# A second level of Strassen's scheme in one projection of a graph attention layer, and a layer norm made in its input's buffer

## The chip, the cores and the metric

The kernel runs on one core of a Trainium2 chip. The metric is device time in microseconds (us), the median over several executions. Engines are named as in the profile: PE is TensorE, PEld its weight load, DVE VectorE, ACT ScalarE, POOL GpSimd, SP SyncE. Where a kernel was timed several times all its runs were in the fast state (a run alone, "one look" below, has no state of its own); the runs of one kernel on one chip agreed within 0.2%.

## The reference, cut to what matters

```python
h = relu(layernorm(x))                       # x: 128 x 64 x 512, fp32
heads = [attend(h, W_heads[i]) for i in 0..3]         # FIRST projection, 4 heads
h1 = elu(concat(heads))                               # 8192 rows x 2048
o  = elu(attend(h1, W_out))                           # SECOND projection, 2048 -> 512
y  = relu(o @ w1 + b1) @ w2 + b2 + o                  # feed forward
out = x + layernorm(y) * gamma + beta
```

`attend` multiplies by the weights, makes a 64x64 softmax from scores and mixes the rows with it. The 8192 rows are worked on as 16 groups (0 to 15) of 512.

## The kernel before

Each group's matrix products use one level of Strassen's scheme (Winograd's form): 7 products of half-size blocks in place of 8. The second projection sums each of the 7 over four heads, with a 256-column moving operand:

```python
def project2(g):
    slot = {1: "11", 2: "12", 3: "12", 4: "22", 5: "S1", 6: "11", 7: "S1"}
    ...
    def post(what, a, b=None, to=None):
        behind = {"s1": ("11", "S1", "11"), "s5": ("S1", "22", "11"), "c11": ("12", "12", "11")}
        if what in behind:                     # the next operands, in place, behind a product
            dst, x0, x1 = (h1[n] for n in behind[what])
            for h in range(H):
                nc.gpsimd.tensor_tensor(dst[:, h], x0[:, h], x1[:, h], ALU.subtract)
        ...
    return unit(f"b{g}", product_n(ms, lambda p, i: h1[slot[p]][:, i]), post, (1, 5, 6, 2, 7, 3, 4))
```

While TensorE does that, the program mixes three other jobs in: the layer norm of group g+2, the z products (softmax weights times rows) of group g+1, and the feed forward of group g-1. Their small steps go through all engines.

```python
rstd = ...; nc.gpsimd.tensor_tensor(rstd, ve, mhalf, ALU.pow)            # A: 1/sqrt of a variance, GpSimd
nc.scalar.activation(HN[t], X.pop(t), AF.Relu, bias=nb, scale=rstd)      # B: layer norm, ScalarE, needs A
nc.scalar.copy(dst, srcv)                                                # C: z out of PSUM, ScalarE
nc.vector.scalar_tensor_tensor(y, y, rstd, xr, ALU.mult, ALU.add)        # D: last norm, VectorE, needs A
eng.tensor_tensor(dst, a, dst, ALU.add)                                  # E: feed forward out of PSUM, VectorE
```

## Time and profile before

| | before |
|---|---|
| median of 3 runs | 2365.08 us |
| TensorE busy | 98% of the span |
| one group in the steady state | 143.0 us |
| waits of TensorE in the steady state | none |

Busy time in one stretch of 600 us (PE, PEld, DVE, ACT, POOL, then the clock, the DMA share and GB/s):

```profile
PEclk7999999999999999999999999999999999999999
```

```profile
L639 DVE SCALAR_TENSOR_TENSOR jf<-wh,ao 128x512 f32<-128x512 f32 x128 | 94.3, 776 | 40.3 <-ACT wh L621 40.1
```

```profile
1000.00:1600.00 600.00, 600.00 (x3078) 503.06 (x3078) 331.60 (x561) 233.62 (x417) 257.56 (x224) 1.00 0.46 151
```

TensorE never pauses in the stretch, and its clock is full after the start. GpSimd works 257.56 of 600 us, 43%. VectorE is 55% busy.

### The profile page before, as it was taken

The numbers are of one execution on the slowest core, as the hardware profiler recorded it, in microseconds if no ns is written. First come the engines' busy times: TensorE is split into PE (matmuls) and PEld (weight loads), VectorE is DVE, ScalarE is ACT, GpSimd is POOL, SyncE is SP. The second block draws the span as 40 slices with busy tenths as digits, with TensorE's granted clock in tenths as the row PEclk, the third lists the DMA queues.
The fourth block names the chain that finished last, engine by engine and source line by source line (L and its number), as shares of the span: only waits on it lengthen the run. The fifth ranks groups of instructions, "written<-read, shape, count | busy, mean of one in ns | idle before, by whom it ended". The sixth has DMA issues, their size and how long they took to land.

```text
span 2360.4 us, 32849 instructions
## 1 busy us (share of the span) xinstructions
PE 2317.9 (98%) x11805; PEld 1934.5 (82%) x11805; DVE 1265.5 (54%) x2210; ACT 911.0 (39%) x1623; POOL 1026.7 (43%) x917
## 2 busy tenths in 40 slices
PE   6989999999999999999999999999999999999997
PEld 4868787888878888787887878888788887878885
DVE  7625474554646556474554745556464563744527
ACT  2524425253352533425244251533525344251513
POOL 5664444416344353443524444253443534533333
PEclk7999999999999999999999999999999999999999
DMA  8545353444535445353444544435354453534443
GB/s 308 184 142 193 125 183 127 164 152 132 182 125 178 134 139 179 126 180 129 154 163 129 182 131 161 153 130 181 127 177 132 138 179 127 182 118 164 157 148 106
DMA packets 257809, 366.89 MB, mean 155 GB/s; under 512 B 22216, under 2 KB 145128, under 8 KB 257648
## 3 DMA queue, kind: packets, MB, share of 16 engines
q1 hardware_dynamic: 251024, 343.82, 43.9%
q0 software_dynamic: 4512, 16.78, 1.9%
q10 hardware_dynamic: 2112, 4.19, 0.5%
q8 instruction: 95, 1.56, 0.3%
q14 instruction: 66, 0.54, 0.1%
HBM read 337.45 MB, written 27.26 MB: 155 GB/s over the span
## 4 chain that ended last, share of the span: by engine, by line
PE 94%; DVE 2%; ACT 1%; POOL 1%; issue 0%; DMA 0%; DVEq 0%
PE g_b L322 33%; PE g_a L307 32%; PE g_c L307 8%; PE g_d L322 8%; PE pz L525 4%; PE pa L673 2%; PE pto L700 1%; PE pzS L525 1%; PE pth L371 1%; PE s1pt L472 1%; PE pf L381 1%; PE s1pe L406 1%; DMA x<-in_x_dram 0%; PE s2pt L667 0%; PE pwa L193 0%
## 5 line engine op out<-in xcount | busy, mean ns | idle before, releaser
L322 PE MATMUL g_b<-w,h 128*128 128x256 f32 x2560 | 598.1, 381 | 0.0
L322 PEld LDWEIGHTS g_b<-w,h 128*128 128x128 f32 x2560 | 480.5, 190 | 72.2 <-issue 10.1
L307 PE MATMUL g_a<-z,w 128*128 128x256 f32 x1520 | 361.0, 380 | 1.2 <-DVE g_a L581 0.7
L307 PE MATMUL g_a<-zs_z,w 128*128 128x256 f32 x1504 | 347.9, 379 | 0.0
L307 PEld LDWEIGHTS g_a<-z,w 128*128 128x128 f32 x1520 | 287.6, 190 | 57.9 <-issue 14.3
L307 PEld LDWEIGHTS g_a<-zs_z,w 128*128 128x128 f32 x1504 | 284.8, 190 | 50.5 <-issue 14.3
L322 PE MATMUL g_b<-w,hS 128*128 128x256 f32 x1024 | 243.5, 382 | 0.0
L585 POOL TENSOR_TENSOR hS<-hS,h 128x512 f32<-128x512 f32 x64 | 83.0, 1297 | 366.8 <-DVE hS L549 366.8
L547 ACT ACTIVATE exc<-g_a 128x512 f32<-128x512 f32 x256 | 152.3, 595 | 199.7 <-DVE g_a L581 119.6
L322 PEld LDWEIGHTS g_b<-w,hS 128*128 128x128 f32 x1024 | 191.4, 191 | 30.9 <-issue 6.7
L549 DVE SCALAR_TENSOR_TENSOR h<-exc,g_a 128x512 f32<-128x512 f32 x192 | 131.6, 686 | 136.3 <-ACT exc L548 136.2
L548 ACT ACTIVATE exc<-exc 128x512 f32<-128x512 f32 x256 | 161.6, 631 | 6.5
L615 POOL TENSOR_TENSOR h<-h,h 128x512 f32<-128x512 f32 x64 | 86.7, 1362 | 138.1 <-PE g_b L322 138.0
L332 POOL TENSOR_TENSOR zs_z<-zS,z 128x512 f32<-128x512 f32 x63 | 89.7, 1424 | 128.3 <-PE g_a L307 123.7
L615 POOL TENSOR_TENSOR h<-hS,h 128x512 f32<-128x512 f32 x64 | 81.1, 1268 | 142.4 <-PE g_b L322 142.4
L474 ACT COPY at<-s1pt 128x512 f32<-128x512 f32 x64 | 34.7, 588 | 279.8 <-PE s1pt L472 279.8
L307 PE MATMUL g_c<-ot,w 128*128 128x256 f32 x512 | 123.9, 385 | 0.8 <-DVE n2ve L347 0.8
L322 PE MATMUL g_d<-w,rt 128*128 128x256 f32 x512 | 121.5, 380 | 1.7 <-DVE o L740 1.0
L307 PE MATMUL g_a<-zS,w 128*128 128x256 f32 x496 | 117.2, 379 | 0.0
L639 DVE SCALAR_TENSOR_TENSOR jf<-wh,ao 128x512 f32<-128x512 f32 x128 | 94.3, 776 | 40.3 <-ACT wh L621 40.1
L333 POOL TENSOR_TENSOR zs_z<-z,zs_z 128x512 f32<-128x512 f32 x63 | 85.4, 1357 | 61.1 <-PE g_a L307 40.7
L307 PEld LDWEIGHTS g_c<-ot,w 128*128 128x128 f32 x512 | 93.9, 190 | 21.8 <-issue 9.3
(159 smaller groups left out, 3535.6 us busy)
## 6 DMA issues: line engine op xcount, KB each, us to landing
w<-tc SPq DMA_DIRECT2D x632, 256.0 KB, 2.6
w<-in_L_gnn_W_heads_dram SPq DMA_DIRECT2D x192, 256.0 KB, 2.7
w<-in_L_gnn_W_out_dram SPq DMA_DIRECT2D x192, 256.0 KB, 2.7
w<-in_L_gnn_w_dram SPq DMA_DIRECT2D x96, 256.0 KB, 2.7
x<-in_x_dram SPq DMA_DIRECT2D x66, 256.0 KB, 3.6
xr<-in_x_dram SPq DMA_DIRECT2D x64, 256.0 KB, 2.8
out_dram<-o SPq DMA_DIRECT2D x64, 256.0 KB, 2.1
tc<-pt POOLq DMA_DIRECT2D x20, 512.0 KB, 5.6
```

The lines of the kernel that those rows point to most:

```text
L307: nc.tensor.matmul(bk[:, o, :], w[:, k, ts(o, P)], a[:, k, :], start=start and o == 0 and k == 0, stop=k == 1, skip_group_check=True,)
L322: nc.tensor.matmul(bk[:, j, :], a[:, k, ts(j, P)], w[:, k, :], start=start and k == 0 and j == 0, stop=i == len(ms) - 1 and k == 1, skip_g ...
L332: eng.tensor_tensor(s2, s1, a11, ALU.subtract)
L333: eng.tensor_tensor(s4, a12, s2, ALU.subtract)
L525: nc.tensor.matmul(banks[b][:, c, :].rearrange("p (h n) -> p h n", h=H), src[rows, off + c * P:off + (c + 1) * P], at[rows, b], start=True ...
L547: nc.scalar.activation(ex, src, AF.Relu, scale=-1.0)
L548: nc.scalar.activation(ex, ex, AF.Exp, scale=-1.0)
L549: nc.vector.scalar_tensor_tensor(dst, ex, -1.0, src, ALU.add, ALU.max)
L585: nc.gpsimd.tensor_tensor(dst, dst, H1["22"][:, h], ALU.add)
L615: nc.gpsimd.tensor_tensor(dst[:, h], x0[:, h], x1[:, h], ALU.subtract)
L639: nc.vector.scalar_tensor_tensor(junk, WH2[g][:, j], 1.0, ao[:, c, :], ALU.mult, ALU.mult, accum_out=f[:, c, j:j + 1],)
L673: nc.tensor.matmul(pa, AT2[g][:, j, :], WH2[g][:, j, :], start=True, stop=True)
```

## The change

The intent: in groups 3 to 15 each of the 7 products of the second projection is itself done by Strassen's scheme, 49 products of 128x128 blocks in place of 56. That saves an eighth of TensorE's streaming there. It costs sums: differences of quarter blocks of h1 in every group, sums of the result, and, once, sums of the blocks of W_out (made on GpSimd in groups 1 to 3, stored to HBM). To make room, the layer norm is written over x in x's own buffer.

```diff
-        HN[t] = big.tile([P, F], FP, tag="hn", name=f"hn{t}", bufs=G)
-        nc.scalar.activation(HN[t], X.pop(t), AF.Relu, bias=nb, scale=rstd)
+        HN[t] = X.pop(t)
+        nc.scalar.activation(HN[t], HN[t], AF.Relu, bias=nb, scale=rstd)
...
+    def block_sums(p, i):                       # once: groups 1 to 3, 14 units
+        ... two loads of y on GpSimd's queue
+        nc.gpsimd.tensor_tensor(t[:, 0], y12, y11, ALU.subtract)
+        ... three more, and a store
...
+            if g >= DEEP and h == H - 1:        # half sums of h1, 4 a group
+                for n in {"c11": ["11"], "c12": ["12"], "c21": ["S1", "22"]}.get(what, []):
+                    q = H1[n][:, :, :, P:]
+                    nc.gpsimd.tensor_tensor(q[:, :, 0], q[:, :, 0], q[:, :, 1], ALU.add)
...
+    def project2_deep(g):
+        outer = (1, 2, 5, 6, 3, 7, 4)
+        halves = ((6, 7, 5), (3, 1, 2, 4))
+        def quarter_sums(p):                    # 21 a group
+            nc.gpsimd.tensor_tensor(q2, x[:, :, 0, P:], x[:, :, 0, :P], ALU.subtract)
+            nc.gpsimd.tensor_tensor(q3, x[:, :, 1, P:], q2, ALU.subtract)
+            nc.gpsimd.tensor_tensor(q4, x[:, :, 1, :P], q2, ALU.subtract)
+        ...
+        def part(p, half, j):                   # one of the 49 products
+            ...
+                    if half == 1:
+                        behind(h1, p)           # the 12 old differences, after outer products 1, 2, 5
+                        if p == 3:
+                            inner(0, nc.gpsimd) # 5 sums of the result's upper half
+                        if p == 4:
+                            inner(1, nc.vector) # and of its lower half
+                if j == 3 and p != outer[-1]:
+                    quarter_sums(outer[outer.index(p) + 1])
...
-                prefetch(2 * p + 2)             # the loads of x move to the last z product that
-                prefetch(2 * p + 3)             # reads the buffer; the norms move later
...
+            if g <= DEEP:
+                ... 14 block_sums spread over the first projections of groups 1 to 3
```

Also, several scratch tiles get one buffer where they had two (`s1`, `s5`, `t`), and the ring of weight pieces has 10 buffers where it had 11.

## The prediction

> **What bounds the kernel now.** I read the page first, then the waits of TensorE, the groups of matmuls with their shapes kept apart, the timeline of two stretches, and busy time by stretch. The page gives the span, the chain and the groups that the change touches:
>
> ```profile
> span 2360.4 us, 32849 instructions
> PE 2317.9 (98%) x11805; PEld 1934.5 (82%) x11805; DVE 1265.5 (54%) x2210; ACT 911.0 (39%) x1623; POOL 1026.7 (43%) x917
> ...
> PE 94%; DVE 2%; ACT 1%; POOL 1%; issue 0%; DMA 0%; DVEq 0%
> ...
> L322 PE MATMUL g_b<-w,h 128*128 128x256 f32 x2560 | 598.1, 381 | 0.0
> ...
> L322 PE MATMUL g_b<-w,hS 128*128 128x256 f32 x1024 | 243.5, 382 | 0.0
> ```
>
> The reader is to see that TensorE is 94% of the chain that ended last, and that the second projection (g_b, 3584 instructions) has no idle time ahead of it. An fp32 product of two 128x128 blocks is two instructions: 16 groups x 7 products x 16 calls = 1792 calls, 3584 records. The waits of TensorE confirm it; the longest are all single ones of the start:
>
> ```profile
> PE pzS L525 <- DVE z L537: 5.5, 1, 5.5
> PE s1pt L472 <- DVE s1A L435: 5.4, 1, 5.4
> PE pab L158 <- DMA ar<-in_L_gnn_a_heads_dram: 5.4, 1, 5.4
> ```
>
> Busy time can't say how fast matmuls stream, since ends are modelled (a mean of 381 ns is longer than their spacing). The timeline can, where chunks of 8 follow each other:
>
> ```profile
> 1201.43 1.70 PEld L307 LDWEIGHTS g_a<-z,w 128*128 128x128 f32 x8
> ...
> 1203.16 1.70 PEld L307 LDWEIGHTS g_a<-zS,w 128*128 128x128 f32 x8
> ...
> 1204.88 1.70 PEld L307 LDWEIGHTS g_a<-z,w 128*128 128x128 f32 x8
> ```
>
> 8 instructions in 1.725 us: 216 ns for 256 columns, with no loss between products. The steady state is therefore pure streaming. The first g_b products of two neighbouring groups start at 956.3 and 1099.25 us: 143.0 us a group.
>
> **What the Trainium skill says.** "TensorE: Matmul & The Clock Gate", Step-by-step, says that the next weights are loaded while this matmul runs, and LDWEIGHTS (loading the stationary operand) that a load costs time by its columns, not by the matmul's width. This decides the case: halving the moving width to 128 columns leaves the weight load as it is, so the load could become the bound. The trace agrees with both, and lets me size it:
>
> ```profile
> 985.41 1.04 PE L371 MATMUL pth<-ident,hn 128*128 128x128 f32 x8
> ...
> 30.31 3.96 PEld L193 LDWEIGHTS pwa<-aT,wT 128*128 128x128 f32 x18
> ```
>
> Transposes of 128 columns: (1.04 - 0.27) / 7 = 109 ns apart, so 128 columns stream in 109 ns. The second line is from the start: full 128-column fp32 weights, but matmuls only 2 wide, so it is the load alone: (3.96 - 0.33) / 17 = 213 ns, at a granted clock of 0.50 in that stretch, 107 ns at full clock. So load and stream are nearly equal at 128 columns; I expect 109 to 111 ns, and the load to stay hidden, just.
>
> "GPSIMD Engine Reference", Specifications, says that GpSimd shares its SBUF interface with VectorE and contends with VectorE's instructions of two SBUF inputs. The trace agrees: the same 128x512 addition takes 1268 ns in one group (L615 h<-hS,h) and 1424 ns in another (L332), the means below.
>
> ```profile
> L615 POOL TENSOR_TENSOR h<-hS,h 128x512 f32<-128x512 f32 x64 | 81.1, 1268 | 142.4 <-PE g_b L322 142.4
> L332 POOL TENSOR_TENSOR zs_z<-zS,z 128x512 f32<-128x512 f32 x63 | 89.7, 1424 | 128.3 <-PE g_a L307 123.7
> ```
>
> "DMA: Bandwidth & Descriptors", Specifications, puts the size from which a descriptor runs at line rate at 512 B. The new pieces of uncombined blocks have runs of exactly 512 B (128 floats); no group of the trace before shows such a load in bulk.
>
> **The change part by part.**
>
> 1. Streaming. Groups 3 to 15 (13 of 16) take the deep form. Before: 112 calls of 256 columns, 224 x 0.216 = 48.4 us a group. After: 49 x 4 = 196 calls of 128 columns, 392 x 0.109 = 42.7 us. Saved: 5.7 us a group, 13 x 5.7 = 74 us. If the load adds 2 ns, 392 x 2 ns x 13 = 10 us of that goes.
>
> 2. GpSimd work in every deep group: 21 sums of quarter blocks (128x512), 4 sums into the H1 quadrants (128x512), 5 inner sums of the results (two of 512, three of 256 elements). At 1.3 us and 0.75 us: 27.3 + 5.2 + 4.8 = 37 us. It is not spread: it falls on the stretch of the second projection. Before, that stretch (first row) has 48.8 us of GpSimd in 91.8 us, the next one only 11.7 in 51.1:
>
> ```profile
> 956.30:1048.10 91.80, 91.80 (x504) 76.14 (x503) 50.76 (x82) 28.38 (x51) 48.80 (x44) 1.00 0.46 153
> 1048.10:1099.20 51.10, 51.10 (x232) 43.54 (x231) 27.36 (x52) 28.31 (x50) 11.69 (x9) 1.00 0.45 149
> ```
>
> So about 86 us of GpSimd in a stretch of about 86 us. Not all of the 48.8 us must end inside it, but GpSimd goes from a helper to nearly the bound there. I followed the order of both engines' instructions through one group with these durations: with 1.3 us a sum GpSimd keeps ahead except at one place, with 1.4 us it also falls behind at the last outer product (1.4 us), with 1.45 us by 2.7 us. I take 0.7 us a group for the late part: 12 x 0.7 = 8 us.
>
> 3. The one place where it is always late: the first inner product of a group needs a difference of quarters of h11, which waits for the last head's ELU and for the sum of h11's quarters. From the trace, the product ends at 1095.96, ELU at 1097.98:
>
> ```profile
> 1094.07 1.89 PE L307 MATMUL g_a<-z,w 128*128 128x256 f32 x8
> 1095.80 3.62 PE L307 MATMUL g_a<-zs_z,w 128*128 128x256 f32 x16
> 1099.25 1.03 PE L322 MATMUL g_b<-w,h 128*128 128x256 f32 x4
> ...
> 1097.29 0.69 DVE L549 SCALAR_TENSOR_TENSOR h<-exc,g_a 128x512 f32<-128x512 f32 x1 [0.70 <-ACT exc L548]
> ```
>
> Two GpSimd sums after it, 2 x 1.3, end at 1100.6, while TensorE wants to start at 1099.25 (third line). 1.4 us, and 0.1 us for the weight load then exposed: 1.5 us x 13 = 20 us.
>
> 4. The last group has no other work for TensorE beside most of its inner products. GpSimd's share there, some 27 (quarters) + 16 (12 old sums of h) + 4 (H1) + 5 (inner) + 5 (bias) = 57 us, meets about 50 us of TensorE: 8 us lost, more than that group saves.
>
> 5. Block sums of the weights, once, in groups 1 to 3: 14 units, each with loads and a store issued on GpSimd, four sums of 256 elements, and a wait for its own load in GpSimd's order: 4 x 0.75 + 4 x 0.7 (an issue cost 0.58 to 0.79 us before) + about 2 us of wait = 8 us, 112 us in all, while the first projection needs its sums z. Its slack is about one head (12 us), so I charge 10 us.
>
> 6. DMA: 49 pieces of 256 KB instead of 28, and 10 buffers instead of 11. Queue 1 moved 343.8 MB at 43.9% of the engines' time: 332 GB/s at full use. A deep group of 86 us takes (49 + 14 + 12) x 0.262 = 19.7 MB, 229 GB/s, or about 70%. The ring still reaches 9 pieces x 0.87 us = 7.8 us ahead, against 2.6 us to landing. No charge.
>
> 7. The first layer norm in x's own buffer removes 2 of 4 small buffers and moves loads; TensorE didn't wait there before, so nothing is gained or lost.
>
> Sum: -74 + 20 + 8 + 8 + 10 = -28 us: 2365 - 28 = **2337 us**.
>
> **The rivals.** (a) The weight load isn't hidden at 128 columns. For it: load and stream are equal, any handover shows. Against: the loads of pwa follow each other without a gap. At 115 ns 31 us go and little gain stays; at 130 ns 107 us go: about 2440 us, slower. (b) GpSimd keeps up everywhere, and the first sum is early enough: then only parts 4 and 5 cost, some 2309 us, 2.4% faster. The slack of GpSimd's idle time before L332 speaks for it, the chain of part 3 against. (c) GpSimd is the bound of the stretch, by contention with VectorE, which gets more additions too: 4 to 6 us a group lost in all, the gain is used up, 2365 us. (d) DMA: runs of 512 B stream at a lower rate and pieces come late; at 1 us a piece the 75 transfers still fit into 86 us, so only the last group would suffer, some 5 us.
>
> **Range and chances.** The gain can't exceed 74 us (2291), and parts 3 and 4 alone take 28 of it, so over 2% (under 2318) needs one of them to fail: 0.20. Rival (c) reaches 2365, a part of (a) also. Eight in ten: 2308 to 2366. Slower by over 2% needs (a) in full: 0.04. Within 2%: 0.76.
>
> **What would show it.** Spacing of the 128-column g matmuls in the timeline: 109 to 111 ns right, 115 or more rival (a). Waits of TensorE: a wait for GpSimd at a difference of quarters, some 13 times 1.5 us at the start of a deep group; none means (b), many over all outer products means (c). GpSimd's busy share in the stretch near 90% or more. A group's period about 143 - 5.7 + 1.5 + 0.7 = 139.5 us. In groups 1 to 3, waits for the sums z on GpSimd, some 10 us. A wait of TensorE for w from DMA would show (d). The prediction is wrong if the period of deep groups stays at 143 us or falls under 138 us.

## The result, and the profile after

| | before | after |
|---|---|---|
| median (4 runs each) | 2364.63 us | 2620.55 us (2619.28 to 2624.04) |
| ratio, 95% interval | | 1.1085 (1.1066 to 1.1105) |
| one deep group, in the steady state | 143.0 us | 160.3 us (157.7 to 162.0) |
| groups 1 and 2 | 143.0, 143.0 us | 165.9, 161.3 us |

A ratio is the mean time of one kernel's runs over that of the other's in the same rounds, so it isn't quite the ratio of the medians in the table. A group's time is measured from the first transpose of o (`pto`) in one group to that in the next, and averaged over nine steady groups.

The change was predicted at 2337 us and made the kernel 10.9% slower. From the page of the kernel after:

```profile
span 2619.1 us, 38669 instructions
PE 2360.9 (90%) x13989; PEld 2037.7 (78%) x13989; DVE 1377.4 (53%) x2314; ACT 928.4 (35%) x1688; POOL 1596.4 (61%) x1405
...
PEclk7999989999999999999999999999999999999999
...
PE 63%; POOL 19%; DVE 9%; issue 6%; ACT 2%; DMA 2%; POOLq 0%; SPq 0%; DVEq 0%; ACTq 0%
...
L743 PE MATMUL g_b<-wq,q 128*128 128x128 f32 x2184 | 307.9, 286 | 41.7 <-POOL q L690 24.6
```

TensorE fell from 94% to 63% of the chain that ended last, and GpSimd holds 19% of it. Yet GpSimd is only 61% busy over all, and the products that read its quarter differences (last line) wait for the difference q only 24.6 us in the whole run, as part 3 of the prediction had it. So where are the other waits? The waits of TensorE (us in total, times, longest):

```profile
PE g_d L380 <- DVE o L901: 81.8, 25, 8.5
PE pz L580 <- ACT z L590: 36.4, 11, 3.4
PE g_b L743 <- POOL q L690: 24.6, 15, 4.0
...
PE s1pe L464 <- POOL R L450: 16.3, 11, 1.5
PE g_b L743 <- POOL n2rs L407: 16.1, 11, 1.6
```

The two largest are not in the projection that was changed, and they don't name GpSimd. They are the second feed-forward product (`g_d`), which waits for VectorE to take a sum out of PSUM (step E), and the z product (`pz`), which waits for ScalarE to do the same (step C). The timeline tells who held these two up. First the z product of one group, all engines (start, length, what; in brackets the idle time before and its releaser):

```profile
1394.77 4.95 POOL L670 TENSOR_TENSOR h<-hS,h 128x512 f32<-128x512 f32 x4 [0.23 <-PE g_b L743]
...
1396.61 1.13 PE L580 MATMUL pz<-at,hn 64*128 64x256 f32 x8
...
1396.84 0.15 DVE L405 TENSOR_SCALAR n1ve<-n1mv 128x1 f32<-128x1 f32 x1
...
1402.12 0.55 POOL L407 TENSOR_TENSOR n1rs<-n1ve,mhalf 128x1 f32<-128x1 f32 x1
...
1403.07 0.81 ACT L417 ACTIVATE hn<-hn,n1nb,n1rs 128x512 f32<-128x512 f32 x1 [5.75 <-POOL n1nb L415]
1403.79 0.56 ACT L590 COPY z<-pz 128x512 f32<-128x512 f32 x1
```

```profile
1404.41 1.13 PE L580 MATMUL pz<-at,hn 64*128 64x256 f32 x8 [3.38 <-ACT z L590]
```

Read it backwards from the last line. TensorE waited 3.38 us for a PSUM bank that ScalarE had to empty. The products to be copied had begun at 1396.61 and lasted 1.13 us, so the copy could have run at 1397.7. It ran at 1403.79, because ScalarE's queue had the layer norm (step B) ahead of it and stood 5.75 us there. Step B needed step A, a half-microsecond instruction whose input was ready at 1396.99 (third line) and which ran at 1402.12. GpSimd was busy all this time: four differences issued in one go (4.95 us), then two further sums. TensorE thus waited for ScalarE, which waited for GpSimd.

The second feed-forward product of the same group, a little later:

```profile
1460.82 1.71 POOL L729 TENSOR_TENSOR wh<-wh 128x512 f32<-128x512 f32 x1 [0.27 <-DVE wh L719]
...
1461.33 0.14 DVE L405 TENSOR_SCALAR n2ve<-n2mv 128x1 f32<-128x1 f32 x1
...
1462.48 1.71 POOL L690 TENSOR_TENSOR q<-h 128x512 f32<-128x512 f32 x1
1464.16 0.72 POOL L730 TENSOR_TENSOR wh<-wh 128x256 f32<-128x256 f32 x1
1464.84 0.55 POOL L407 TENSOR_TENSOR n2rs<-n2ve,mhalf 128x1 f32<-128x1 f32 x1
...
1465.42 1.20 DVE L910 SCALAR_TENSOR_TENSOR o<-o,n2rs,xr 128x512 f32<-128x512 f32 x1 [2.34 <-POOL n2rs L407]
...
1466.55 0.68 DVE L901 TENSOR_TENSOR o<-g_d,o 128x512 f32<-128x512 f32 x1
...
1467.28 3.68 PE L380 MATMUL g_d<-w,rt 128*128 128x256 f32 x8 [5.14 <-DVE o L901]
...
1470.79 2.40 PE L743 MATMUL g_b<-wq,hS 128*128 128x128 f32 x20
```

It is the same pattern through another queue. The variance is ready at 1461.47, step A runs at 1464.84, behind two inner sums of the result and one quarter difference. VectorE stands 2.34 us at step D, and the evacuation E (L901), for which TensorE waits 5.14 us, is queued behind D. Two more things are to be seen here. The first two sums on GpSimd took 1.71 us in place of 1.27, and both overlap work of VectorE. (From 650 to 2300 us none of the 142 sums of this size that ran with VectorE idle took over 1.29 us, and all 116 of 1.65 us or more overlap VectorE. Not every overlap slows a sum.) And the 8 instructions of `g_d` (256 columns each) took 3.68 us after the wait, where 8 of that size took 1.89 us in the timeline before (the prediction's part 3): the clock had been halved. The stretches show both (columns as above; the first is the 600 us that were shown of the kernel before):

```profile
1000.00:1600.00 600.00, 549.26 (x3382) 478.47 (x3383) 309.43 (x518) 226.59 (x415) 368.25 (x308) 0.96 0.58 168
```

```profile
1460.00:1475.00 15.00, 9.86 (x66) 9.01 (x65) 11.41 (x15) 0.00 (x0) 14.65 (x13) 0.89 0.65 183
```

In the 15 us of the second, GpSimd works 14.65 us: it is the bound of that place, though its mean over the 600 us is 61%. ScalarE did nothing at all in them.

The last two lines of the list of waits are 1.5 us a group each. Before `s1pe`, TensorE waits for R, an operand of a later group's scores, which GpSimd makes behind other sums, as it does step A (in this group its input is ready at 1431.74, and R runs at 1434.89, behind a block of four differences and a quarter difference). The other wait is put down to step A (`n2rs`), and wrongly:

```profile
1478.01 0.68 DVE L721 TENSOR_TENSOR wh<-g_b,wh 128x512 f32<-128x512 f32 x1
...
1478.79 1.13 PE L743 MATMUL g_b<-wq,q 128*128 128x128 f32 x8 [1.60 <-POOL n2rs L407]
```

In all 11 of these waits the product of the last outer product starts 0.10 us after the end of VectorE's evacuation L721, and 0.28 us after the end of the step A that the list names. By these times TensorE waits for VectorE, which has score products (`jf`) ahead of L721.

Two passages of the Trainium skill bear on this. "TensorE: Matmul & The Clock Gate", Architectural detail, says that ScalarE and VectorE take their instructions strictly in order, and that only TensorE can draw something ahead (its weight loads). The timelines agree: a copy that was ready at 1397.7 stood 6.1 us behind a layer norm that wasn't. The same page, Part 1, says that the clock is either full or half, and changes in windows of about 3.4 us. The trace agrees with that: all 23 half-clock stretches from 650 to 1940 us lasted 3.4 or 6.8 us.

Where the 258.7 us between the two spans (2360.4 and 2619.1) come from, by the first transposes of o:

| part | us |
|---|---|
| start, up to the first transpose of o (246.3 to 257.9) | +11.6 |
| groups 1 and 2 (143.0 to 165.9 and 161.3) | +41.2 |
| groups 3 to 13, eleven of them, 17.1 each | +188.5 |
| group 14 (135.9 to 140.6) | +4.7 |
| group 15 (77.8 to 88.5) | +10.7 |
| tail (41.9 to 43.5) | +1.6 |

### The profile page after: what moved, and what is told of

Same layout as the page of the kernel before. It is cut to its first block, busy times and chain, and to the rows that moved or that the text cites. A ratio compares the mean times of both kernels' runs of the same rounds, so it can differ in the third digit from the quotient of the medians.

```text
span 2619.1 us, 38669 instructions
## 1 busy us (share of the span) xinstructions
PE 2360.9 (90%) x13989; PEld 2037.7 (78%) x13989; DVE 1377.4 (53%) x2314; ACT 928.4 (35%) x1688; POOL 1596.4 (61%) x1405
## 4 chain that ended last, share of the span: by engine, by line
PE 63%; POOL 19%; DVE 9%; issue 6%; ACT 2%; DMA 2%; POOLq 0%; SPq 0%; DVEq 0%; ACTq 0%
PE g_a L365 27%; PE g_b L743 13%; PE g_c L365 7%; PE g_b L380 4%; PE pz L580 4%; DVE jf L797 3%; POOL q L690 3%; POOL h L670 3%; PE g_d L380 3%; POOL hS L670 2%; PE pa L832 2%; POOL n2rs L407 1%; DVE o L910 1%; PE pth L429 1%; PE s1pt L530 1%
## 5 line engine op out<-in xcount | busy, mean ns | idle before, releaser
L743 PE MATMUL g_b<-wq,q 128*128 128x128 f32 x2184 | 307.9, 286 | 41.7 <-POOL q L690 24.6
L743 PEld LDWEIGHTS g_b<-wq,q 128*128 128x128 f32 x2184 | 278.3, 198 | 73.8 <-POOL q L690 30.5
L743 PE MATMUL g_b<-wq,h 128*128 128x128 f32 x2080 | 277.6, 285 | 0.0
L743 PEld LDWEIGHTS g_b<-wq,h 128*128 128x128 f32 x2080 | 265.3, 200 | 15.6 <-issue 6.3
L380 PEld LDWEIGHTS g_d<-w,rt 128*128 128x128 f32 x512 | 107.2, 219 | 103.6 <-DVE o L901 83.7
L906 POOL TENSOR_TENSOR xr<-xr,bs 128x512 f32<-128x512 f32 x64 | 95.2, 1491 | 114.0 <-DMA xr<-in_x_dram 105.2
L797 DVE SCALAR_TENSOR_TENSOR jf<-wh,ao 128x512 f32<-128x512 f32 x128 | 151.9, 1221 | 22.8 <-POOL wh L733 22.3
L580 PE MATMUL pz<-at,hn 64*128 64x256 f32 x768 | 115.7, 425 | 36.4 <-ACT z L590 36.4
L604 DVE SCALAR_TENSOR_TENSOR hS<-exc,g_a 128x512 f32<-128x512 f32 x64 | 44.0, 688 | 146.3 <-ACT exc L603 146.3
L580 PEld LDWEIGHTS pz<-at,hn 64*128 64x128 f32 x768 | 71.4, 199 | 59.2 <-ACT z L590 38.4
```

What stands on the lines that cost most here:

```text
L380: nc.tensor.matmul(bk[:, j, :], a[:, k, ts(j, P)], w[:, k, :], start=start and k == 0 and j == 0, stop=i == len(ms) - 1 and k == 1, skip_g ...
L580: nc.tensor.matmul(banks[b][:, c, :].rearrange("p (h n) -> p h n", h=H), src[rows, off + c * P:off + (c + 1) * P], at[rows, b], start=True ...
L604: nc.vector.scalar_tensor_tensor(dst, ex, -1.0, src, ALU.add, ALU.max)
L743: nc.tensor.matmul(bk[:, place[j][1]], x[:, h], w[:, h], start=first and h == 0, stop=h == H - 1, skip_group_check=True,)
L797: nc.vector.scalar_tensor_tensor(junk.rearrange("p (c v o) -> p c v o", c=2, v=2), WH2[g][j], 1.0, ao[:, c, :].rearrange("p (c v o) -> p c ...
L906: nc.gpsimd.tensor_tensor(xr, xr, bs, ALU.add)
```

## The experiments

Twelve kernels ran; one more, with step A on VectorE, did not compile, so the order of queues was tested by moving the sums and not by moving step A. Theory: the added GpSimd sums and their place in the static order hold up small GpSimd results (step A, and the inner sums) which ScalarE and VectorE wait for in order, and TensorE waits for those two. Rivals: the deep form itself (its smaller products, its PSUM banks, its weight pieces) costs the time; the in-place layer norm does; or plain load on GpSimd does, whatever its order. In the text, "gap" is idle time of TensorE in a steady group, "clock" the time lost to the halved clock in one (half the length of its half-clock stretches).

| run | total us | a steady group us | gap us | clock us |
|---|---|---|---|---|
| before | 2364.6 | 143.0 | 0 | 0 |
| after | 2620.6 | 160.3 | 14.5 | 6.6 |
| e1 no deep group | 2371.0 | 142.6 | 0 | 0 |
| e2 no quarter differences (wrong result) | 2480.3 | 148.6 | 6.5 | 2.5 |
| e3 differences behind on VectorE | 2552.7 | 155.5 | 11.0 | 5.1 |
| e5 old form and idle sums | 2485.5 | 152.7 | 7.2 | 2.8 |
| e6 block sums alone | 2419.0 | 142.5 | 0 | 0 |
| e7 inner sums on VectorE | 2570.0 | 155.9 | 12.2 | 4.4 |
| e8 three kinds on VectorE | 2490.4 | 150.8 | 8.4 | 2.1 |
| e9 none of the added sums (wrong result) | 2451.5 | 146.4 | 4.7 | 2.1 |
| e10 as e8, scores last | 2486.1 | 150.2 | 9.1 | 0.0 |
| e11 as e9, differences behind on VectorE (wrong result) | 2393.5 | 141.9 | 2.3 | 0.9 |

The kernel before ran at medians of 2363.81 to 2365.26 us beside them, whichever chip it was.

### e1: the rest of the change without the deep form

```diff
-DEEP = 3
+DEEP = 99
...
-            if g <= DEEP:
+            if g <= DEEP < NG:
```

> No group takes the deep form and no block sums are made; the rest of the change stays (layer norm in x's buffer, ring of 10, moved loads and norms). Theory GpSimd queue (the added sums fill GpSimd's in-order queue during the second projection, and VectorE and ScalarE, which wait for its small layer norm results in their own order, release PSUM banks late): 2360 to 2375 us, as before, clock 0.99. Rival rest of the change (fewer buffers, moved norms): over 2420 us.

Measured: 2370.95 us (2369.34 to 2371.2), 1.0027 of the kernel before (1.0010 to 1.0043), result correct. The steady group takes 142.6 us and TensorE has no gap in it. The in-place layer norm and the later norms therefore cost nothing in the steady state. They, or the smaller buffers beside them, cost some 11 us at the start (first transpose of o at 257.4 us in place of 246.3). All the rest of the loss, 2620.55 - 2370.95 = 250 us, hangs on the deep groups and their block sums.

### e2: no differences of quarters

```diff
         def quarter_sums(p):
             x = h1[SLOT[p]]
-            q2, q3, q4 = (...)
-            nc.gpsimd.tensor_tensor(q2, ...)      # and q3, q4
-            QS[p] = {6: q2, 7: q3, 3: q4}
+            QS[p] = {6: x[:, :, 0, P:], 7: x[:, :, 1, P:], 3: x[:, :, 1, :P]}
```

> The deep form without its 21 quarter differences a group: the inner products take plain quarters, so the result is wrong on purpose; TensorE's work, banks, pieces and evacuations stay. Theory GpSimd queue: about 27 of 37 us of added sums a group are gone, period of a deep group 139 to 143 us, total 2300 to 2360 us. Rival banks (the deep form holds six PSUM banks) or rival pieces (DMA of 256 KB per 0.9 us, weight load at 128 columns): the period stays over 152 us, total over 2500 us.

Measured: 2480.27 us, relative error 0.533 as intended. A steady group falls from 160.3 to 148.6 us, gap and clock from 21.1 to 9.0 us. The 21 differences cost 11.7 us a group, although TensorE waits for them directly for only 1.3 us. Their cost lies in what they hold up. The period is in neither range that was expected (139 to 143 us, or over 152): these sums are a large part of the loss, not all of it.

### e3: the twelve old differences on VectorE

```diff
-                nc.gpsimd.tensor_tensor(dst[:, h], x0[:, h], x1[:, h], ALU.subtract)
+                nc.vector.tensor_tensor(dst[:, h], x0[:, h], x1[:, h], ALU.subtract)
```

> The 12 outer differences of h a group go from GpSimd to VectorE (in all groups). Theory GpSimd queue: 15 us a group leave GpSimd, 8 us come to VectorE, whose share is under 0.6: period falls from 160 to 146-152 us, total 2430 to 2520 us. If the port that both share, or VectorE itself, is what is short (rival VectorE): no gain or slower than 2620 us. Rivals banks and pieces: within 20 us of 2620.

Measured: 2552.72 us, correct. The z product's wait for ScalarE is gone from the list (3.3 us a group before). This shows the chain of the first timeline: it was the four differences ahead of step A. The wait for E is now 6.0 us a group, where it had been 5.3: VectorE got the work, and E stands behind it. The period of 155.5 us misses the 146 to 152 us that were expected.

### e5: the old form with as much load on GpSimd

```diff
-DEEP = 3
+DEEP = 99
...
+        def idle_sums(what, x):                  # 28 a group, read by nobody
+            for i in range(4 if g >= 3 else 0):
+                q = wk.tile([P, 2, T], FP, tag=f"q{2 + i % 3}", ...)
+                nc.gpsimd.tensor_tensor(q, x, x, ALU.add)
...
+                idle_sums(what, a)               # after each outer product's evacuation
```

> No deep group; instead 28 sums a group of 128x512 whose results nobody reads are added on GpSimd in groups 3 to 15, each four after the evacuation of one outer product: 36 us a group, as the deep form adds. Theory GpSimd queue: the load alone slows the old form by 5 to 15 us a group, total 2430 to 2560 us, with waits of TensorE for PSUM evacuations and clock under 0.98. Rival: GpSimd's load does no harm without the data that TensorE needs from it: 2365 to 2385 us.

Measured: 2485.52 us, correct. Its stretch from 1000 to 1600 us:

```profile
1000.00:1600.00 600.00, 572.08 (x2885) 478.94 (x2884) 322.23 (x528) 215.48 (x393) 372.96 (x323) 0.98 0.44 142
```

GpSimd works 372.96 us of 600, as it does after the change (368.25). The same old products, nothing read from the idle sums, and a group takes 152.7 us in place of 142.6. Load on GpSimd, on the old banks and pieces, makes the same waits: `g_d` for VectorE's o 3.5 us a group, `pz` for ScalarE's z 1.8 us. That rules out the deep form's PSUM banks and weight pieces as a necessary cause. It makes 10 of the 22 us (160.3 against the ideal of 138.1 that is worked out under e9). The idle sums come four at a time, so this run doesn't tell load from blocks.

### e6: the block sums alone

The deep form is off and the block sums of groups 1 to 3 are on; the order of products is the old one.

```diff
-        second = project2_deep if g >= DEEP else project2
+        second = project2
```

> Only the block sums of the weights in groups 1 to 3, no deep group (nobody reads their result). If they are what lengthens groups 1 and 2 by 41 us together: 2405 to 2425 us, with periods of the first two groups near 165 and 161 us and the later ones at 142.5 us. Rival: those groups are slow for the new buffers, then as the run without any deep form, 2371 us.

Measured: 2419.01 us, correct. Groups 1 and 2 take 165.4 and 160.8 us, that is 41 us more than in e1; all later groups take 142.5 us. So the block sums account for the whole of the loss in groups 1 and 2, and the prediction had 10 us for them. (Its first transpose of o comes at 264.6 us, 7 us later than in e1. I read nothing from that: in the kernel after, e2, e7 and e9, which run the same instructions up to there, it comes between 257.9 and 261.7 us.) Two lines of GpSimd show the place:

```profile
344.30 0.72 POOL L280 TENSOR_TENSOR ty<-y 128x256 f32<-128x256 f32 x1 [2.64 <-DMA y<-tco]
...
345.67 0.56 POOL L407 TENSOR_TENSOR n2rs<-n2ve,mhalf 128x1 f32<-128x1 f32 x1
```

GpSimd stood still 2.64 us for the block sum's own load with step A queued behind it. TensorE had an 8.41 us gap up to 348.13, before `g_d`, released by E, which came after D, which came after this step A. The prediction had looked for this loss at the first projection's sums z; it is again the feed forward.

### e7: the upper inner sums on VectorE

```diff
-                            inner(0, nc.gpsimd)
+                            inner(0, nc.vector)
```

> The whole change, but the inner sums of the upper result half on VectorE instead of GpSimd. If VectorE's products for the scores, queued ahead of the feed-forward's evacuation, wait for exactly these sums on GpSimd, the longest wait (TensorE for VectorE's addition into o, 5.1 us in every deep group) falls by more than half: period 151 to 156 us, total 2500 to 2560 us. If only GpSimd's total counts: 5 of 37 us go, 156 to 159 us, total 2570 to 2610 us.

Measured: 2570.04 us, correct; 155.9 us a group. The wait of `g_d` for E fell from 5.3 to 2.4 us a group, which shows the second timeline: the inner sums on GpSimd were in E's way. But the wait for VectorE's evacuation L721 rose from 1.5 to 2.9 us a group (the list names it "issue" here; see e8), so the total misses the theory's 2500 to 2560 us and lies on the edge of the 2570 to 2610 that were expected if only GpSimd's total counts. It is the wait, which fell by more than half, that speaks for the theory.

### e8: inner sums, differences behind and the feed forward's sums on VectorE

```diff
-                nc.gpsimd.tensor_tensor(dst[:, h], x0[:, h], x1[:, h], ALU.subtract)
+                nc.vector.tensor_tensor(dst[:, h], x0[:, h], x1[:, h], ALU.subtract)
...
-                            inner(0, nc.gpsimd)
+                            inner(0, nc.vector)
...
-            eng = nc.vector if what[0] == "c" else nc.gpsimd
-            eng.tensor_tensor(dst, a, dst, ALU.add)
+            nc.vector.tensor_tensor(dst, a, dst, ALU.add)
```

> The whole change with three kinds of sums moved from GpSimd to VectorE: the 12 outer differences of h, the inner sums of the upper half, and the two additions into o: 22 us a group leave GpSimd, 12 us come to VectorE. Theory GpSimd queue: gaps and clock loss fall below a third of 21 us, period 140 to 146 us, total 2370 to 2450 us. Rival banks: gaps stay over 10 us a group, total over 2500 us.

Measured: 2490.38 us, correct, against the 2370 to 2450 us that I hoped for: a miss. 150.8 us a group. The largest gap (2.8 us a group) was a product of the projection with no releaser in the list. In the timeline it begins at 1413.75, just after VectorE's evacuation L721 (1412.98, 0.67 us long) into the same PSUM block; L721 had three score products (`jf`, 0.69 to 1.37 us), an evacuation of `g_d` and a 1.28 us statistic ahead of it. VectorE had become what GpSimd was. Gap and clock are 10.5 us, between the two ranges expected. This reading is from times, since the trace names no releaser.

### e9: none of the added sums

As e2, and also without the four half sums and the upper inner sums:

```diff
-            if g >= DEEP and h == H - 1:
+            if False and h == H - 1:
...
-                        if p == 3:
-                            inner(0, nc.gpsimd)
```

> The deep form with every sum that it adds to GpSimd left out (quarter differences, sums into h, inner sums of the upper half), so the result is wrong on purpose; TensorE's instructions, banks, evacuations, pieces and the block sums of groups 1 to 3 stay. If GpSimd's added sums are the whole cost: period 138 to 140 us (142.5 less 4.4 of streaming), total 2355 to 2385 us, the excess over 2312 being the block sums. If six banks or late pieces cost by themselves: period 144 us or more, with waits of TensorE for evacuations or DMA left.

Measured: 2451.52 us, relative error 0.587 as intended; expected were 2355 to 2385 us, a miss that told the most. (The rival's "144 us or more", by six banks or late pieces, fits the period; e11 decides against it.) The period of the rest of the change without the deep form (142.5 us in e6) less the gain in streaming, 4.4 us (worked out in the next section), is 138.1 us; e9 takes 146.4. GpSimd here has less to do than before the change:

```profile
1000.00:1600.00 600.00, 580.50 (x3669) 510.68 (x3668) 327.28 (x577) 240.22 (x440) 244.18 (x213) 0.98 0.62 184
```

```profile
PE pz L580 <- ACT z L590: 23.0, 11, 2.2
```

244.18 us of 600, against 257.56 before. Yet TensorE still waits 2.1 us at the z product in each deep group. So load isn't the whole cause; the order is the other part. The twelve old differences follow outer products 1, 2 and 5 in both forms. In the traces of the kernel before and of e1 they run on GpSimd one or two at a time, with other work between them (72 alone and 18 pairs in nine groups before). In the deep form they run four in one go, 4.96 us, in all 27 blocks of nine groups of the kernel after, and one such block lies just ahead of a step A. (In this run one is at 1331.58 to 1336.54, the variance is ready at 1334.23, and step A runs at 1337.73, after one sum more of 1.26 us.) No run put the deep form's differences apart again, or changed the order of the outer products or of the feed forward's products alone, which the deep groups also have new.

### e11: as e9, with the twelve differences on VectorE

```diff
-                nc.gpsimd.tensor_tensor(dst[:, h], x0[:, h], x1[:, h], ALU.subtract)
+                nc.vector.tensor_tensor(dst[:, h], x0[:, h], x1[:, h], ALU.subtract)
```

> The run without the added sums (146.4 us a group, wrong on purpose), and the 12 outer differences of h on VectorE as well. In that run GpSimd is only 0.41 busy, yet TensorE still waits 2.1 us a group for ScalarE's copies of z, which stand behind a layer norm activation, which waits for small results that stand behind four differences on GpSimd. If the order in the queues is the cause and not GpSimd's total: the wait for ScalarE's copy is gone, period 143 to 145 us, total 2405 to 2435 us. If GpSimd's order has nothing to do with it: the wait stays, total within 10 us of 2451.

Measured: 2393.49 us, better than the 2405 to 2435 expected. 141.9 us a group, 4.5 less than e9, and the wait of `pz` is gone; what leads the waits now is a transposition that waits for VectorE's softmax:

```profile
PE s1pt L530 <- DVE s1A L493: 28.1, 12, 5.4
PE g_d L380 <- DVE o L893: 16.9, 4, 7.1
```

So these twelve differences, where they stand, cost 4.5 us a group even with no added sum on GpSimd. And it sets a limit: without any of the added sums, with a wrong result, this program still needs 2393 us, more than the kernel before, though some 41 us of that are the block sums (e6).

The traces also hold the delay of step A itself, from the end of the instruction that makes its variance to its start (mean and longest of 36 in nine steady groups). For the layer norm B: 0.5 and 1.8 us in e1, 2.6 and 5.4 in the kernel after, 1.2 and 4.1 in e9, 0.1 and 0.3 in e11. For the last norm D: 0.3 and 1.0 us in e1, 0.9 and 3.4 in the kernel after, 0.10 and 0.15 in e7, 4.4 and 5.1 in e5. The delay comes and goes with the sums, as the theory has it.

### e10: as e8, with the scores after the last inner sum

```diff
+            if g >= DEEP and j == 0:
+                tc.add_manual_dep(first.ins, LAST["inner"].ins.name, ...)
```

> The run with three kinds of sums on VectorE, and the scores' products on VectorE made to follow the last inner sum, so that they can't stand in VectorE's queue ahead of the evacuations of the second projection and of the feed-forward. If that order is what keeps 8.4 us of gaps a group: gaps under 5.5 us, period 145 to 148 us, total 2410 to 2465 us. If VectorE's load itself is the bound: within 15 us of 2490.

Measured: 2486.11 us, correct, 4 us under e8, where 2410 to 2465 were expected: a miss, and inside the range of the rival, that VectorE's load is the bound (within 15 us of 2490). The wait that e8's list names "issue" has not gone: it fell from 2.8 to 1.5 us a group. The list names step A for it, but in all 11 cases the product starts 0.10 us after VectorE's L721 ends, as in the kernel after. Beside it stand waits for an evacuation by ScalarE (1.4) and for the first quarter difference (1.3), none long. All gaps together are a little larger than in e8, 9.1 us, but the clock was never halved. I come back to that in the last section. Some 3 us of its period stay unexplained (142.5 - 4.4 + 9.1 = 147.2 against 150.2).

### e12 and e13: the start

Does the start lose its 11 us to x's buffers? e12 is e1 with seven of them in place of four. Or to the scratch tiles that lost their second buffer? e13 is e1 with two of each again.

```diff
-            tl = big.tile([P, F], FP, tag="hn", name=f"hn{t}", bufs=G)
+            tl = big.tile([P, F], FP, tag="hn", name=f"hn{t}", bufs=G + 3)
```

> No deep form and no block sums, as the first run of this study (steady period 142.5 us against 143.0 before, but some 11 us lost ahead of group 1), with 7 instead of 4 buffers for x and its layer norm. If the loss at the start comes from x's loads waiting for buffers that group 0 still reads: 2357 to 2364 us, 0.1 to 0.3% faster than before. If it comes from elsewhere: 2368 to 2373 us.

```diff
-        aT = wk.tile([P, H, 2, KC], FP, tag="s1", name="aT", bufs=1)
+        aT = wk.tile([P, H, 2, KC], FP, tag="s1", name="aT")
...
-                junk = wk.tile([P, O], FP, tag="t", name=f"jk{c}_{m}_{k}", bufs=1)
+                junk = wk.tile([P, O], FP, tag="t", name=f"jk{c}_{m}_{k}")
...
-                    [P, 2, T], FP, tag=nm, name=f"{nm}_{name}", bufs=1
+                    [P, 2, T], FP, tag=nm, name=f"{nm}_{name}"
```

> This is the run without any deep group, but with two buffers again, as in the kernel before, for the evacuated sums s1, s5 and t of a product, the fold's scratch and the folded vectors (the change left one of each). Theory A: the 11 us lost at the start come from the second buffers that were taken away: then TensorE's first transpose of o comes at 248 us or earlier instead of 257.4, and the total is 2361 to 2365 us, equal to the kernel before or a little under it, since a period of 142.5 instead of 143.0 us gives some 7 us back over 14 groups. Theory B: the loss has another source (order of the start's work on VectorE and GpSimd, or where the clock's windows fall): the first transpose stays at 255 to 260 us and the total at 2369 to 2373 us.

Measured: e12 2371.58 us (1.0030 of before, 1.0016 to 1.0044), first transpose of o at 259.7 us: x's buffers are not it. e13 2367.28 us (1.0015, 1.0002 to 1.0029), first transpose at 252.4 us against 257.4 in e1. Neither of e13's two theories holds whole: the second buffers seem to give back some 4 to 5 us, and 6 us stay. That isn't shown clear of noise: the two intervals overlap, and the first transpose moves by up to 7 us between single profiles of kernels that run the same instructions up to there (e6). Where the rest goes is open. The trace of e13 shows the first product with a sum z on VectorE waiting 2.9 us, against 1.0 us before, and what orders that I didn't test.

A version that beats the kernel before was not found. The gain in streaming is 4.4 us in each of 13 groups, 57 us. The block sums took 41 of them (e6) and the wait for the first quarter difference 1.3 x 13 = 17. Those two alone use the gain up, before any of the waits above.

## Why the prediction was wrong, point by point

**Part 1, streaming: the mechanism right, the size off.** In the second timeline 20 instructions of 128 columns took 2.40 us; less the 0.28 us length of the last, 2.12 / 19 = 112 ns apart, where 109 (at most 111) was assumed. 392 x 0.112 = 43.9 us against 48.4, thus some 4.5 us a group in place of 5.7 (4.4 is used in this text), and 57 us in all in place of 74. The load of the weights stays hidden: rival (a) is out.

**Part 3, the first inner product: right.** 1.5 us a group was predicted. 1.3 us was measured, 24.6 us in 15 waits, of which one was 4.0 us long.

**Part 2, GpSimd in the deep groups: this is the step that failed.** The prediction put the added load right: it sits where TensorE works on the second projection, and GpSimd is the bound of some places (its share there was to be near 90%; from 1383.9 to 1490 us it worked 79.7 of 106.1 us, 75%, since the stretch got longer). But it "followed the order of both engines' instructions", GpSimd's and TensorE's, and charged "0.7 us a group for the late part". Two engines were missing from that walk. TensorE waits little for GpSimd itself, 1.3 us a group for the first quarter difference (part 3) and 1.5 us for R. ScalarE and VectorE wait, in their order, for half-microsecond results that stand behind those sums on GpSimd, and TensorE waits for what is queued behind them. In the place of 0.7 us stand 14.5 - 1.3 = 13.2 us of waits a group: 8.6 at `g_d` and `pz`, the two chains shown, 1.5 each for R and for L721, and some 1.6 that I didn't follow. A second term was left out wholly: after some of the waits the clock is halved, 6.6 us a group. The account of a group closes within 1.1 us: 142.5 - 4.4 + 14.5 + 6.6 = 159.2, measured 160.3.

The experiments divide the loss over the ideal of 138.1 us in this order of removal: 11.7 us go with the quarter differences (e2), 2.2 with half sums and inner sums (e9), 4.5 with the twelve old differences off GpSimd (e11), and 3.8 remain. In another order of removal the parts would differ, since the waits hide one another. What I didn't separate is the slower pace of VectorE and GpSimd when both work: the group `jf`, shown of before with a mean of 776 ns, has 1221 ns after.

**Part 4, the last group: sign right, size off.** (Its own numbers, 57 against 50, make 7 us.) A loss of 8 us less the 5.7 saved there was predicted, about 2 us; it was 10.7 us, and 4.7 in the group before. In e2, without the quarter differences, the last group takes 74.9 us, 2.9 less than before the change: it does save once GpSimd has room.

**Part 5, the block sums: mis-sized, and in the wrong place.** 41 us in place of 10 (e6), although it charged four issues a unit where the program has three. "Its slack is about one head" held for the sums z. It said nothing about the step A of the feed forward, which shares GpSimd's queue.

**Part 6, DMA: right.** No wait for a weight piece is among the large ones, and the DMA share is 0.58.

**Part 7, layer norm in place: right for the steady state** (e1: 142.6 us and no gap), wrong by 11 us for the start, of which the second buffers of scratch tiles hold perhaps 4 to 5 (e13).

**The rivals and the range.** Rival (c), "GpSimd is the bound of the stretch", had the direction. It gave 4 to 6 us a group and would have shown as waits at all outer products; it was 20 us and showed at `g_d` and `pz`. With 0.04 for slower, the chances were far too sure: both queues that failed were visible in the profile before, in step D and B's place in the program, and were not looked at.

## What to carry to other kernels

On engines that work strictly in order, ask of each piece of added work not only who reads its result, but which small results stand behind it in its queue, and who stands waiting for them: follow at least one chain through all engines to a PSUM bank. A mean busy share of 61% says little if the work falls in blocks of 5 us in front of half-microsecond steps. And a matmul engine that pauses a few us can lose nearly half as much again to its clock (6.6 us beside 14.5 in the kernel after, but nothing beside 9.1 in e10).

## What the Trainium skill lacked or had wrong

- "TensorE: Matmul & The Clock Gate", HAM oscillation, warns of idle gaps of TensorE over about 3.4 us. Here shorter ones were often followed by a half-clock stretch: of the waits between 1.75 and 2.5 us in e9, 12 of 16 were (by one that began between 0.5 us before the wait and 3.6 us after it), in the kernel after 7 of 7 between 2.5 and 3.5 us. But none of 10 between 1.75 and 2.5 us was in e7, and in e10, where no steady wait was over 2.5 us, none of 80 (of 0.15 us or more). The page's next section tells of frequent short pauses that also do it, without a length; which of them count stays open here. Counted from 650 to 1940 us of each trace.
- The same page, Back-to-back issue gap, has no spacing for fp32, nor have other pages. Here fp32 products of 128 columns, each with its own weight load, are 112 ns apart for each of their two instructions, and those of 256 columns 216 ns.
- "GPSIMD Engine Reference", Specifications, names the contention with VectorE but gives no size ("SBUF — State Buffer", Who interferes with whom, has one, GpSimd 1.5 times slower, without its instructions). Here a 128x512 sum took 1.27 us in most places and 1.71 to 1.72 us in many places beside VectorE's score products; those took 1.74 us there and 0.65 us at their fastest (in e8).
